# Other estimates and other ranks for the scheduler of a fused transformer kernel

## The chip, the cores and the metric

The kernel runs on one core of a Trainium2 chip. One core has five engines that run their own queues of instructions in order: TensorE (PE, the matrix products), VectorE (DVE), ScalarE (ACT), GpSimd (POOL) and SyncE (SP, which only starts transfers). They meet through semaphores. Sixteen DMA engines move data between the chip's memory and the core. The metric is the device time of one execution in microseconds; of several runs the median is taken.

## The reference

A batch of 16 sequences of 256 tokens of width 128 goes through four layers. Each layer adds a gated cross attention and then a gated feed-forward part to `x`:

```python
x = x + jnp.tanh(g_xattn[0]) * _L0_xattn_ref(_layernorm(x, axis=-1), ctx_1024, ctx_1024, ...)
x = x + jnp.tanh(g_ffn[0]) * _L0_ffn_ref(_layernorm(x, axis=-1), ...)
...
```

- The attentions have 16 heads of width 8 and 64 context tokens. The first takes its softmax over the heads, the others over the context; the second adds a bias for each batch (`fside`) and a mask, the third and the fourth have masks.
- Feed-forward 0 is a mixture of eight experts (128 to 512 to 128, with gelu): each token goes to its two best experts, and a shared expert is added. Feed-forward 1 is a ternary 128x128 matrix. Feed-forward 2 comes down to one expert, the second of its sixteen. Feed-forward 3 is a mixture of eight experts in which each token goes to its best one.

All products are in float32.

## The kernel before

**Halves and stages.** The batch is split in two halves of eight sequences (called half 0 and half 1 here; sequences 0 to 7 and 8 to 15). Each half goes through eight stages: attention 0, mixture 0, attention 1, ternary, attention 2, expert 2, attention 3, mixture 3. The halves share nothing but buffers, so that one half's attention (much DVE work) can run beside the other's mixture (PE and transfers).

**Mixtures.** Tokens are sorted by expert into tiles of 128 rows: 39 tiles for each half in mixture 0 (two experts for a token, and room for a part tile of each expert), 23 in mixture 3. `sorted_pair` (L1901) handles two tiles: fetch the rows (`xg`; in mixture 0 POOL's indirect gather, L1927; in mixture 3 a plain transfer from SP, L1922), transpose them (PE, L1941), copy to `xgT` (DVE, L1945), first product for each tile (PE, L1955), gelu (ACT, L1962), second product (PE, L1976), bias (DVE, L1986), and a store. In mixture 0 the store goes to `ysort` in memory (SP, L2008), from which `collect` (L2036) gathers two rows for each token by POOL (`yg`, L2045) and adds them on DVE (L2053). In mixture 3 an indirect scatter writes the kernel's output (POOL, L2021). `fetch` (L1883) loads each tile's expert, 578 KB, from SP (L1896) into one of six buffers `wb`; a buffer is free when DVE's bias (L1986) of the tile that used it is done.

**Regions.** Mixture 3 scatters the normalised tokens into regions of a table in memory, one for each expert (`last_mixture`, `block`, POOL, L1752), and that table is written with a fill pattern before: `fill_regions` (L1872) issues 27 transfers of 645 KB for each half from SP (L1877). A half's scatters wait for all 27 of its fills. Attention 1 loads its `fside` tile for each sequence in `make_fill1` (L1061, the transfers at L361), also from SP, into one of three buffers. POOL carries small steps of attentions 2 and 3 (`mx`, L1200 to L1203) and of the layer normalisation (`ln`, L738 to L741) as well.

**What sets the order.** No order is written out. Every piece of work is a Python generator that yields requests: `op(engine, length, *needs)`, `dma(queue, size, *needs)` or `get(slots, number, *needs)` for buffers. `Order.run` (L223) takes, again and again, the request that could begin first by its estimates. Begin times are rounded to 0.1 us, and among equal ones the lowest rank wins. The instructions are issued in that order on PE, DVE, ACT, POOL and SP. So the estimates, all in microseconds, decide the order, and nothing of them is executed:

- `REACH` is added where a need comes from another engine; a transfer ends at `max(wire, at + LAND) + size / RATE`, so that all transfers share one wire.
- `RANKS` (L96) has one row for each half and one rank for each of the eight stages; `rank` (L2063) adds a little for each sequence. The shared expert has its mixture's rank plus 0.6, and `collect` its plus 0.1. Constants have rank 50 and the region fills 100.

**Fillers.** Where the scheduler sees PE idle, `keep_busy` (L206) puts in products of the identity whose result nobody reads (`spin`, L471, 128x512 in bfloat16): as many as bring the last 3.4 us of its own timeline to a share of 0.85, each counted as 0.22 us.

```python
                self.wire = max(self.wire, at + LAND) + size / RATE
...
        want = min(room, max(SHARE * min(WINDOW, end) - busy, SHARE * (end - begin - WINDOW)))
        while want > 0 and t < end - SPIN:
            if not self.spin(t):
                return
```

Of the kernel before, what the change touches and what calls it, by code (L numbers as in the profile page):

```python
# [84 lines left out]

PE, DVE, ACT, POOL, SP = "PE", "DVE", "ACT", "POOL", "SP"

REACH, LAND, RATE, SWAP = 0.1, 1.8, 280e3, 1.3
INF = float("inf")


# [1 line left out]

TURNED = (1,)

RANKS = ((4, 10, 2, 10, 1, 7, 1, 16), (15, 10, 3, 16, 5, 13, 12, 16))  # L96


class Event:
# [18 lines left out]
class Order:  # L118
# [33 lines left out]
    def give(self, slot, slots, at):  # L152
        slot.at = at
        slots.free.append(slot)
# [104 lines left out]
def op(engine, length, *needs, table=None):  # L259
    return ("op", engine, length, needs, table)  # L260


def dma(queue, size, *needs):
    return ("dma", queue, size, needs, None)


def get(slots, number, *needs):
    return ("get", slots, number, needs, None)
# [24 lines left out]
def flamingo_kernel(  # L293
# [1028 lines left out]
    def two(slot):  # L1322
        return slot.ap[:, 0:1024].rearrange("p (a b) -> p a b", a=2)
# [82 lines left out]
    def first_mixture(hf, rank, begin, end):  # L1406
# [231 lines left out]
        for q in range((n + 1) // 2):  # L1638
            needs = (indexed, kept)
            order.task(  # L1640
                rank + 0.001 * q,
                sorted_pair(l, hf, q, st, ex, needs, room[q], fetched[q], stored),
            )
# [4 lines left out]
    def last_mixture(hf, rank, begin):  # L1648
# [167 lines left out]
        for q in range((n + 1) // 2):  # L1816
            order.task(
                rank + 0.001 * q,
                sorted_pair(
                    l, hf, q, st, ex, (at, kept), room[q], fetched[q], None, filled, empty  # L1820
                ),
            )
# [78 lines left out]
    def sorted_pair(l, hf, q, st, ex, needs, room, fetched, stored, filled=None, empty=None):  # L1901
# [13 lines left out]
        for i in range(m):  # L1915
            if l == 3:
# [4 lines left out]
                at = yield dma(SP, 132e3)  # L1921
# [3 lines left out]
            at = yield op(POOL, 1.3, *xgs, *needs)  # L1925
# [9 lines left out]
        if l == 0:  # L1935
            at = (at[0] + 3.0, "DMA")
        (xgT,) = yield get(xgT_s, 1)
        (pt,) = yield get(banks, 1)
        pe = at = yield op(PE, 0.11 * m, at, pt)
# [4 lines left out]
        at = yield op(DVE, 0.17 * m, at, xgT)  # L1944
# [4 lines left out]
        hts = []  # L1949
        for i in range(m):  # L1950
            (ph,) = yield get(banks, 1)
            pe = yield op(PE, 0.9, at, ph, fetched)
            for c in range(NF):
                cs = slice(c * P, (c + 1) * P)
                nc.tensor.matmul(  # L1955
                    ph.ap[:, cs], wb[i].ap[:, cs], xgT.ap[:, i * P : (i + 1) * P],
                    start=True, stop=True,
                )
            ht = yield op(ACT, 1.15, pe, hb, table=table)
            for c in range(NF):  # L1960
                cs = slice(c * P, (c + 1) * P)
                nc.scalar.activation(  # L1962
                    two(hb)[:, i, cs], ph.ap[:, cs], func,
                    bias=wb[i].ap[:, PK_B1 + c : PK_B1 + c + 1],
                )
            give(ph, banks, ht)
            hts.append(ht)
# [3 lines left out]
        place = y.ap[:, 2 * D :].bitcast(I32)  # L1971
        (py,) = yield get(banks, 1)
        for i in range(m):
            at = yield op(PE, 0.9, hts[i], py)
            for c in range(NF):
                nc.tensor.matmul(  # L1976
                    py.ap[:, i * D : (i + 1) * D],
                    two(hb)[:, i, c * P : (c + 1) * P],
                    wb[i].ap[:, PK_W2 + c * D : PK_W2 + (c + 1) * D],
                    start=(c == 0),  # L1980
                    stop=(c == NF - 1),
                )
# [23 lines left out]
        if l == 0:  # L2006
            at = yield dma(SP, 65e3 * m, yt)
# [10 lines left out]
        for i in range(m):  # L2018
            at = yield op(POOL, 1.41, yt)
# [10 lines left out]
        at = (at[0] + 3.0, "DMA")  # L2030
# [32 lines left out]
    def rank(stage, hf, i=0):  # L2063
        return RANKS[hf][stage] + 0.01 * i

# [128 lines left out]
```

## Time and profile before

| | |
|---|---|
| median of 14 runs | 1002.89 us (999.21 to 1009.87) |
| the profiled execution | 1006.01 us, of which the span is 1004.3 us |
| PE busy | 916.5 us, 91% of the span |
| DVE, POOL, ACT busy | 666.5, 629.4, 571.4 us |
| mean granted clock of PE | 0.96 |
| transfers | 150.19 MB, 150 GB/s over the span |
| fillers | 175 products |

How to read it: a row of the instruction views gives the start, the duration, the engine, the line in the kernel, what is written and read, the number of merged instructions, and in brackets how long the engine was idle just before and who ended that. Products in the trace are pipelined: the next begins before the one before has ended, so that a duration is longer than the step from one to the next. A row of the stretches gives, for a window of time, the busy time of each engine, the clock granted to PE and what the transfers moved. A float32 product is two entries of the trace.

### The profile page before, as it was taken

What the parts mean: (1) busy time and instruction counts of PE and PEld (TensorE: products, weight loads), DVE (VectorE), ACT (ScalarE), POOL (GpSimd) and SP (SyncE); (2) the same over time, 40 slices, a digit from 0 to 9 for tenths busy, and PEclk for the clock granted to TensorE, in tenths of its full rate; (3) what the DMA queues carried; (4) which work ended last, traced back from release to release, by engine and by line L of the source; (5) the groups of instructions that cost most, each with busy time, mean ns of one, the idle gap of its engine ahead of it and who ended that gap; (6) DMA issues with size and microseconds to landing.
All of it is one profiled execution on the core that took longest, in us unless ns stands there. A gap on an engine that the chain in (4) does not pass through costs nothing.

```text
span 1004.3 us, 28746 instructions
## 1 busy us (share of the span) xinstructions
PE 916.5 (91%) x10775; PEld 719.7 (72%) x10775; DVE 666.5 (66%) x2019; ACT 571.4 (57%) x1359; POOL 629.4 (63%) x1031
## 2 busy tenths in 40 slices
PE   6999968989988999999799989999789999998996
PEld 3777746889876998776567667676566667886875
DVE  5889895574356224578597888789567688765342
ACT  5654324576454446667358558665655776783433
POOL 5798755679762577677458756425286566756443
PEclk9998878999989999999799999999989999999998
DMA  7000004557874689451643940099995014557983
GB/s 212 3 3 24 23 1 143 169 180 232 248 194 164 230 276 351 156 133 46 131 117 83 197 102 2 15 230 219 219 214 136 1 42 162 158 183 266 302 293 124
DMA packets 96428, 150.19 MB, mean 150 GB/s; under 512 B 11298, under 2 KB 75945, under 8 KB 96289
## 3 DMA queue, kind: packets, MB, share of 16 engines
q1 hardware_dynamic: 88304, 131.77, 46.1%
q0 software_dynamic: 7552, 15.65, 6.0%
q8 instruction: 85, 1.39, 0.6%
q10 hardware_dynamic: 432, 0.93, 0.4%
q14 instruction: 55, 0.44, 0.1%
HBM read 99.11 MB, written 50.12 MB: 149 GB/s over the span
## 4 chain that ended last, share of the span: by engine, by line
PE 22%; DVE 7%; SPq 7%; DMA 5%; POOL 4%; issue 3%; ACT 2%; POOLq 0%; DVEq 0%; ACTq 0%
SPq L1877 6%; PE bank L1955 4%; PE bank L1976 3%; DMA xg<-xrow 2%; PE bank L1271 2%; PE bank L1104 2%; DVE mx L1189 2%; DMA yg<-ysort,state 2%; PE bank L1230 2%; PE bank L1293 1%; PE bank L872 1%; DMA xrow<-rows_sb 1%; PE bank L838 1%; PE bank L1238 1%; PE bank L1382 1%
## 5 line engine op out<-in xcount | busy, mean ns | idle before, releaser
L1962 ACT ACTIVATE big<-bank,wb 128x128 f32<-128x128 f32 x496 | 137.4, 384 | 123.1 <-issue 76.0
L1955 PE MATMUL bank<-xgT,wb 128*128 128x128 f32 x992 | 130.9, 281 | 5.7 <-DVE xgT L1945 3.6
L1955 PEld LDWEIGHTS bank<-xgT,wb 128*128 128x128 f32 x992 | 120.7, 195 | 16.8 <-DVE xgT L1945 12.3
L1976 PE MATMUL bank<-wb,big 128*128 128x128 f32 x992 | 125.3, 277 | 0.0
L747 ACT ACTIVATE xn<-x,ln 128x128 f32<-128x128 f32 x224 | 93.7, 492 | 49.9 <-POOL ln L741 49.8
L1976 PEld LDWEIGHTS bank<-wb,big 128*128 128x128 f32 x992 | 119.0, 193 | 1.8 <-issue 0.9
L1927 POOL DMA_INDIRECT xg<-xrow,state x78 | 76.2, 977 | 40.1 <-PE bank L1832 22.6
L1189 DVE TENSOR_REDUCE mx<-bank 128x8 f32<-128x512 f32 x128 | 80.4, 683 | 16.8 <-PE bank L1110 15.9
L1258 ACT ACTIVATE pT<-bank 128x512 f32<-128x512 f32 x128 | 67.2, 606 | 41.1 <-PE bank L1245 38.5
L2045 POOL DMA_INDIRECT yg<-ysort,state x64 | 62.8, 981 | 42.5 <-DVE x L2053 16.9
L990 POOL TENSOR_TENSOR pT<-pT,rc 128x1024 f32<-128x1024 f32 x32 | 75.2, 2373 | 18.8 <-DVE rc L985 14.0
L1986 DVE TENSOR_TENSOR y<-bank,wb 128x128 f32<-128x128 f32 x124 | 32.4, 287 | 80.2 <-PE bank L1976 75.3
L768 POOL TENSOR_TENSOR x<-x,rows_sb 128x256 f32<-128x256 f32 x96 | 71.7, 765 | 14.8 <-ACT xn L747 14.2
L738 POOL TENSOR_SCALAR ln<-ln 128x4 f32<-128x4 f32 x64 | 14.7, 230 | 99.3 <-DVE ln L736 89.4
L2021 POOL DMA_INDIRECT out_dram<-y x46 | 46.8, 1017 | 46.5 <-DVE y L1986 37.2
L735 DVE BATCH_NORM_STATS2 ln<-x 128x6 f32<-128x128 f32 x256 | 68.9, 269 | 5.1 <-DMA x<-in_x_dram 4.8
L1104 PE MATMUL bank<-kexp,qT 32*128 32x256 f32 x768 | 68.4, 415 | 2.2 <-DVE x L1330 2.0
L739 POOL TENSOR_TENSOR ln<-ln,mhalf 128x4 f32<-128x4 f32 x64 | 66.9, 1045 | 5.3
L1945 DVE COPY xgT<-bank 128x256 f32<-128x256 f32 x64 | 25.9, 412 | 58.2 <-PE bank L1941 47.6
L1271 PE MATMUL bank<-pT,vx 128*32 128x256 f32 x768 | 59.0, 395 | 0.2 <-ACT pT L1258 0.2
L736 DVE BATCH_NORM_AGGREGATE ln<-ln 128x2 f32<-128x6 f32 x256 | 46.6, 182 | 9.7
L1142 DVE TENSOR_REDUCE mx<-bank 128x8 f32<-128x512 f32 x64 | 43.5, 682 | 13.6 <-PE bank L1110 13.5
(273 smaller groups left out, 2174.7 us busy)
## 6 DMA issues: line engine op xcount, KB each, us to landing
wb<-in_pk_l_dram SPq DMA_DIRECT2D x124, 578.0 KB
xrow<-rows_sb SPq DMA_DIRECT2D x54, 645.0 KB
xg<-xrow SPq DMA_DIRECT2D x46, 129.0 KB
ysort<-y SPq DMA_DIRECT2D x38, 128.0 KB
fill<-in_fsideT_dram SPq DMA_DIRECT2D x64, 64.0 KB
x<-in_x_dram SPq DMA_DIRECT2D x16, 128.0 KB
xrow<-xn SPq DMA_DIRECT2D x8, 256.0 KB
xg<-xrow,state POOLq DMA_INDIRECT x78
```

The costliest lines, as they stand in the source:

```text
L735: nc.vector.bn_stats(st[:, 2 * i + j, :], xs[b][:, j, :])
L747: nc.scalar.activation(xn[:, k, :], xs[b][:, j, :], AF.Identity, bias=nm[:, k : k + 1], scale=rs[:, k : k + 1],)
L768: nc.gpsimd.tensor_tensor(xs[b], xs[b], row.unsqueeze(1).to_broadcast([P, 2, D]), ALU.add)
L990: nc.gpsimd.tensor_tensor(s3, s3, rc.ap.unsqueeze(1).to_broadcast([P, 8, P]), ALU.mult)
L1104: nc.tensor.matmul(dst(g), qT[strip(g), ts], kexp[strip(g)].rearrange("p h k -> p (h k)"), start=True, stop=False,)
L1189: nc.vector.tensor_reduce(mx[:, :, g, :], sc[g].ap.rearrange("p (t h k) -> p t h k", h=4, k=S2), AX.X, ALU.max,)
L1258: nc.scalar.activation(pTs[g // 2].ap[:, (g % 2) * 512 : (g % 2 + 1) * 512], sc[g].ap, AF.Exp)
L1271: nc.tensor.matmul(po.ap[strip(g), i * S : (i + 1) * S], vx.ap[:, b % 2, c, :], pTs[c // 4].ap[:, (c % 4) * S : (c % 4 + 1) * S], start=Tr ...
L1927: nc.gpsimd.indirect_dma_start(out=xg[i], out_offset=None, in_=xd, in_offset=bass.IndirectOffsetOnAxis(ap=index[:, 2 * q + i : 2 * q + i + ...
L1955: nc.tensor.matmul(ph.ap[:, cs], wb[i].ap[:, cs], xgT.ap[:, i * P : (i + 1) * P], start=True, stop=True,)
L1962: nc.scalar.activation(two(hb)[:, i, cs], ph.ap[:, cs], func, bias=wb[i].ap[:, PK_B1 + c : PK_B1 + c + 1],)
L1976: nc.tensor.matmul(py.ap[:, i * D : (i + 1) * D], two(hb)[:, i, c * P : (c + 1) * P], wb[i].ap[:, PK_W2 + c * D : PK_W2 + (c + 1) * D], st ...
```

## The change

Three things change, all of them numbers that only the scheduler reads. `REACH` goes from 0.1 to 0.3, `LAND` from 1.8 to 2.0 and `RATE` from 280 to 270 KB for each microsecond. The length of a tile's first product in `sorted_pair` goes from 0.9 to 1.0 and of its second from 0.9 to 0.97. Seven of the sixteen ranks change: in half 0 those of attention 0, mixture 0, attention 1 and expert 2, in half 1 those of attention 1, attention 2 and mixture 3. The computation, the buffers, the transfers and their sizes stay as they are; the order of the instructions on each engine and the number and places of the fillers come out otherwise.

```diff
-REACH, LAND, RATE, SWAP = 0.1, 1.8, 280e3, 1.3
+REACH, LAND, RATE, SWAP = 0.3, 2.0, 270e3, 1.3
...
-RANKS = ((4, 10, 2, 10, 1, 7, 1, 16), (15, 10, 3, 16, 5, 13, 12, 16))
+RANKS = ((11, 14, 1, 10, 1, 9, 1, 16), (15, 10, 6, 16, 12, 13, 12, 14))
...
             (ph,) = yield get(banks, 1)
-            pe = yield op(PE, 0.9, at, ph, fetched)
+            pe = yield op(PE, 1.0, at, ph, fetched)
...
         for i in range(m):
-            at = yield op(PE, 0.9, hts[i], py)
+            at = yield op(PE, 0.97, hts[i], py)
```

## The prediction

> **What bounds the kernel now.** First the page, for the engine that is full; then stretches of the span, for where it is not; then the rows around the idle places. The page and the fillers' own line:
>
> ```profile
> PE 916.5 (91%) x10775; PEld 719.7 (72%) x10775; DVE 666.5 (66%) x2019; ACT 571.4 (57%) x1359; POOL 629.4 (63%) x1031
> PEclk9998878999989999999799999999989999999998
> L478 PE MATMUL bank<-ident x175: 376/379/634, 1.4 to 989.5; 128*128 128x512 bf16 x175
> ```
>
> PE is the bound: 87.8 us of the span are not busy, and its clock has a few low slices. What is computed on it does not change, so the change can move three things only: idle PE, stretches at half clock, and fillers. The stretches (columns: busy PE, weight loads, DVE, ACT, POOL with their counts, granted clock, transfer share, GB/s):
>
> ```profile
> 100.00:160.00 60.00, 44.30 (x574) 32.89 (x559) 53.59 (x108) 15.58 (x30) 35.58 (x37) 0.79 0.06 17
> 230.00:300.00 70.00, 62.90 (x664) 57.60 (x663) 28.62 (x99) 38.38 (x112) 54.27 (x65) 0.93 0.73 220
> 300.00:400.00 100.00, 96.22 (x776) 84.66 (x775) 39.42 (x112) 50.24 (x150) 58.78 (x95) 0.98 0.75 253
> 400.00:500.00 100.00, 88.15 (x935) 69.04 (x935) 66.09 (x175) 60.66 (x138) 65.89 (x117) 0.93 0.47 123
> 700.00:760.00 60.00, 51.84 (x713) 36.43 (x712) 38.75 (x126) 35.60 (x79) 33.72 (x68) 0.91 0.94 216
> 890.00:1004.30 114.30, 99.28 (x754) 83.35 (x752) 51.56 (x243) 48.70 (x165) 58.68 (x95) 0.98 0.70 234
> ```
>
> From 100 to 160 DVE is the bound (routing of mixture 0, 53.6 of 60). From 230 to 500 run the experts of mixture 0 and the gathers behind them: 22.7 us of PE idle. At 700 to 760 there is one hole, and after 890 mixture 3 alone, with 15 us idle. The rest is packed. The rows of the two holes, by engine:
>
> ```profile
> 474.98 3.75 SPq L1877 DMA_DIRECT2D xrow<-rows_sb  x4
> 485.03 0.35 DVE L2053 SCALAR_TENSOR_TENSOR x<-yg,state,x 128x128 f32<-128x128 f32 x1 [4.83 <-DMA yg<-ysort,state]
> 486.76 0.95 PE L1168 MATMUL bank<-ident,pT 128*128 128x128 f32 x4 [3.23 <-DVE pT L1150]
> 725.72 1.12 POOL L1752 DMA_INDIRECT xrow<-big,state  x1 [8.82 <-DMA xrow<-rows_sb]
> 730.67 0.40 PE L1212 MATMUL bank<-identb,mx 128*128 128x128 bf16 x2 [6.97 <-POOL mx L1203]
> ```
>
> First hole: four region fills enter the transfer queues at 475, the gathers behind them land late, DVE waits 4.83 us in its order, and PE waits for DVE. Second hole: POOL waits 8.82 us for the regions to be filled, attention 2's small POOL steps stand behind it, PE waits 6.97 us. The rows of the end:
>
> ```profile
> 891.89 0.71 PE L872 MATMUL bank<-wa,oT 128*128 128x128 f32 x4 [0.25 <-ACT oT L1316]
> 918.13 1.00 POOL L1752 DMA_INDIRECT xrow<-big,state  x1 [0.16 <-issue]
> 930.33 1.49 SPq L1922 DMA_DIRECT2D xg<-xrow  x2
> 941.46 2.10 PE L478 MATMUL bank<-ident 128*128 128x512 bf16 x9
> 943.09 1.52 SPq L1896 DMA_DIRECT2D wb<-in_pk_l_dram  x2
> 943.17 0.42 DVE L1945 COPY xgT<-bank 128x256 f32<-128x256 f32 x1
> 943.64 2.05 PE L1955 MATMUL bank<-xgT,wb 128*128 128x128 f32 x16
> 948.06 1.49 SPq L1896 DMA_DIRECT2D wb<-in_pk_l_dram  x2
> 951.67 1.95 PE L1955 MATMUL bank<-xgT,wb 128*128 128x128 f32 x16
> 953.46 2.08 PE L1976 MATMUL bank<-wb,big 128*128 128x128 f32 x16
> 955.74 0.33 PE L1941 MATMUL bank<-ident,xg 128*128 128x128 f32 x1 [0.20 <-DMA xg<-xrow]
> ```
>
> The last attention ends at 892.6, its tokens are scattered by 919.1, and half 1's first rows are fetched at 930.33, since half 0's tiles are still in front in SP's order. A pair of tiles then takes 4.97 us of SP's order (943.09 to 948.06).
>
> **Do the new numbers fit the rows better?** Partly. Two first products begin 1.79 us before the next thing (951.67 to 953.46): 0.895 us for a tile, which is 0.9 and not 1.0. DVE's copy ends at 943.59 and PE begins at 943.64: 0.05 us of way, nearer to 0.1 than to 0.3. Transfers go the other way: the pair whose experts are issued at 948.06 has its rows on PE at 955.74, 7.68 us for 2 x 578 + 2 x 129 KB; the old numbers make 1.8 + 1414/280 = 6.85, the new 2.0 + 1414/270 = 7.24. So three of the numbers move away from the trace and two towards it: this alone decides nothing, and the order must be read.
>
> **The change part by part.** The two sources, built, give the order of every engine (counts, no times). Counts of work are the same on DVE and ACT; POOL issues 4 more separators (L521, 0.21 us each, beside its idle 37%: nothing, or 0.9 us if its queue is full there).
>
> 1. *Fillers before the end of half 1's attention 3*: 83 become 143, and 45 of the 60 stand among mixture 0's experts (32 become 77). In a run a filler steps by (2.10 - 0.38) / 8 = 0.215 us, so 60 cost 12.9 us if PE had no idle there, and nothing if each lies in a wait. The 45 need 9.7 us, and 22.7 us are idle in 230 to 500, but the new ones stand in runs of one to nine at almost every pair, where the old trace shows packed products. I take half: **+6** (0 to 12.9; 15.8 by 46.0 us / 175).
> 2. *Five tiles of half 0's mixture 3 move ahead of the end of attention 3* (first products left behind it: 13 become 8). 5 x 2 x 0.9 = **+9** before that end; from 760 to 890 PE has only 2.1 us idle, so 7 at least.
> 3. *The end after attention 3*: SP's order is 2.5 pairs shorter, 12.4 us, but half 1's rows can't be fetched before their scatters land. They are issued by 919.1, 11.2 us before 930.33, less some 3 us to land: **-8** (0 to -11.2). Fillers there: 92 become 103, 11 x 0.215 = 2.4, in part in waits: **+1**.
> 4. *First hole*: the first fills now stand behind the mask load of the fourth layer's keys (L789, which before waited for ACT until 506) instead of behind half 0's last fside load, and 15 instead of 22 of half 1's gathers are issued after them. The hole costs 3.23 + 2.40 us of waits and 10.2 us at half clock, 10.7 in all. But the next groups of fills are 5 and 9 instead of 3 and 6, 5 x 3.2 us = 16 of transfers before the same loads. I take **-4** (-10.7 to +5).
> 5. *Second hole*: 20 instead of 21 fills stand before half 0's table is full. In the trace they run from 651.58 to 725.72; one less is 3.2 us, so 70.9, and the scatter and the small steps behind it 2 us: 73. PE has 85 steps and 6 fillers between the release of that group and the blocked step, instead of 95 and none: at 75.2/95 = 0.79 us, 68.5, less 3.1 for the loads ahead of the fills, 65.4. The hole is 7.6 us instead of 7.0: **+1** (-7 to +8). What is queued on POOL behind the wait is again an attention's small steps, now of attention 3.
> 6. *Start of mixture 0*: 14 more DVE instructions, 8.6 us by their rows, come before its first bias, in the stretch where DVE is full; PE has 15.7 us idle there and other work: **+2** (0 to 8.6).
>
> Everything else in the order moves work that PE does anyway. Sum: 6 + 9 - 8 + 1 - 4 + 1 + 2 = +7. The profiled execution took 1006.0 us, 3.1 above the median, and so 1013.0 by its own time, **1010 for the median**.
>
> The second hole shows what an idle PE costs beyond itself: from 725.9 to 736.2 the granted clock is 0.5. A rule that speaks against this forecast: the Trainium skill, "TensorE: Matmul & The Clock Gate", section "Why this matters for your kernels", advises against PE gaps of over about 3 us, since an idle window puts the array back to half clock. The trace agrees with it in that row. By the rule the new fillers in mixture 0 would pay: without half clock from 230 to 400, and with their 6 us for nothing, the sum would be about -6.
>
> **The rivals.**
> - *The fillers fall into waits and hold the clock (faster).* Place: mixture 0, 230 to 400. For it: 0.93 and 0.98 granted there, 0.07 x 70 + 0.02 x 100 = 6.9 us lost, and 10.9 us idle. Against it: those low slices come from single waits of up to 3.3 us for gathered rows, not from many short ones. Sum: 7 - 6 - 6.9 = -6, so 997. It decides as soon as fillers cost under 0 net, with term 4 as taken.
> - *The first hole goes (same).* With the gathers clear of the fills all 10.7 us are saved instead of 4: sum 0, 1003.
> - *The larger groups of fills hit attention 1 (much slower).* Nine fills before the fside loads of half 1's last sequences hold them 3 x 3.2 = 9.6 us longer, and a hole of that size costs 5 us of half clock again: 1025. For it: POOL already waits up to 5.5 us for such a load. Against it: those loads wait for buffers (16 us at 554) longer than for the wire.
> - *Nothing changes*: excluded, since the order differs on all engines.
>
> **How the numbers follow.** Forecast 0.45, own range 1006 to 1017; faster rival 0.28; first hole 0.12; larger groups 0.15. Two runs of this kernel can be told apart from about 0.3%, 3 us. Faster 0.28, same 0.12, slower 0.60 (the forecast and the larger groups). The range takes in the faster rival with the first hole half gone as well and the larger groups with term 1 at its bound: 990 to 1030.
>
> **What would show it.** Fillers: busy PE from 230 to 500 up by about the fillers' time, with idle down by less. End: the last L872 near 905 of the span or later, and at most 107 us after it. First hole: no DVE wait of 4 us for `yg` beside a group of L1877, and clock 1.0 from 487 to 497. Second hole: one POOL wait for `xrow` of 8 to 10 us and one PE wait of 7 to 8. The forecast is wrong if idle PE outside the end falls by more than the 13 us of new fillers, or if a new hole of over 5 us stands in attention 1.

## The result and the profile after

The changed kernel takes 1039.37 us (median of 13 runs, 1035.87 to 1043.53), the kernel before 1005.09 us (median of 62 runs); the ratio is 1.0346, with an interval of 1.0325 to 1.0367. The forecast was 1010 with a range of 990 to 1030: the sign is right, and the loss of about 34 us is five times the 7 us of the sum. The profiled execution of the changed kernel spans 1036.1 us, 31.7 more than before.

The page after, in its rows of busy time and granted clock and in the fillers' own row:

```profile
PE 942.6 (91%) x10846; PEld 739.0 (71%) x10846; DVE 674.9 (65%) x2019; ACT 570.0 (55%) x1359; POOL 627.1 (61%) x1035
PEclk9999779998999999999889989999999999999998
L478 PE MATMUL bank<-ident 128*128 128x512 bf16 x246 | 67.4, 396 | 1.6 <-POOL hmask L403 1.4 <-DVE pT L1150 0.2
```

PE's share is 91% as before, and its busy time has grown by 26.1 us, of which 21.4 carry the name of the fillers. A first reading is that the fillers ate the time. The experiments below refute it: when the fillers are taken out, the time stays.

The same six stretches as in the prediction (busy PE, weight loads, DVE, ACT, POOL with counts, granted clock, transfer share, GB/s); the last runs to the new end:

```profile
100.00:160.00 60.00, 45.42 (x595) 32.48 (x595) 55.15 (x112) 21.09 (x37) 35.00 (x37) 0.80 0.13 39
230.00:300.00 70.00, 64.39 (x582) 56.01 (x583) 32.15 (x92) 34.14 (x100) 53.90 (x64) 0.93 0.74 228
300.00:400.00 100.00, 92.88 (x726) 81.39 (x724) 34.38 (x103) 46.61 (x145) 49.23 (x82) 1.00 0.68 224
400.00:500.00 100.00, 89.54 (x891) 72.79 (x895) 64.19 (x170) 59.91 (x139) 71.39 (x118) 0.94 0.57 152
700.00:760.00 60.00, 56.80 (x696) 40.44 (x689) 48.06 (x148) 37.70 (x82) 21.27 (x44) 1.00 1.11 222
890.00:1036.05 146.05, 130.59 (x1146) 110.64 (x1144) 71.63 (x315) 75.30 (x220) 77.94 (x129) 0.97 0.67 215
```

Clock times shift, so stretches between equal clock times compare different work. A better comparison counts the pieces of work that the scheduler gives to PE, in order (992 in each kernel, fillers left out; the first product of a tile is one piece, for example), and takes the start of the piece with the same number in both traces. The orders differ, so the work behind a number isn't always the same, and pieces differ in length: a few us of the lead can be other work. The lead of the kernel before, in us:

| piece | 160 | 240 | 400 | 440 | 680 | 720 | 880 | last product of attention 3 | end of span |
|---|---|---|---|---|---|---|---|---|---|
| after less before | -4 | +4 | +12 | +12 | +32 | +23 | +31 | +40 | +32 |

The last tile of mixture 0 is piece 401 before and 388 after; from 440 to 680 stand the attentions of both halves, with the last gathers of half 1. There the loss is largest. From piece 400 to piece 600 both kernels do nearly the same work on PE (2039 entries of the trace before, 2026 after, and 7 and 21 fillers). The two stretches, before and then after, columns as above:

```profile
458.60:635.40 176.80, 164.05 (x2046) 116.18 (x2044) 141.32 (x420) 113.52 (x245) 113.67 (x219) 0.97 0.43 95
```

```profile
470.90:665.00 194.10, 173.97 (x2047) 124.40 (x2047) 140.25 (x398) 109.00 (x233) 114.94 (x218) 0.94 0.39 85
```

The 17.3 us more are, by estimate, 7.4 of idle PE (176.80 - 164.05 = 12.75 becomes 194.10 - 173.97 = 20.13) and some 6 of lower clock (0.03 x 176.8 = 5.3 becomes 0.06 x 194.1 = 11.6); 14 more fillers make another 3. What PE waits for is seen in the rows of SP, DVE and PE, in order of time:

```profile
480.98 0.35 SPq L789 DMA_DIRECT2D xf<-in_mask_dram  x1
481.38 4.02 SPq L1877 DMA_DIRECT2D xrow<-rows_sb  x4
522.21 5.00 SPq L1877 DMA_DIRECT2D xrow<-rows_sb  x5
584.79 17.36 SPq L1877 DMA_DIRECT2D xrow<-rows_sb  x9
```

```profile
492.30 0.35 DVE L2053 SCALAR_TENSOR_TENSOR x<-yg,state,x 128x128 f32<-128x128 f32 x1 [4.93 <-DMA yg<-ysort,state]
534.96 0.35 DVE L2053 SCALAR_TENSOR_TENSOR x<-yg,state,x 128x128 f32<-128x128 f32 x1 [3.75 <-DMA yg<-ysort,state]
602.02 0.35 DVE L2053 SCALAR_TENSOR_TENSOR x<-yg,state,x 128x128 f32<-128x128 f32 x1 [5.18 <-DMA yg<-ysort,state]
```

```profile
494.45 1.09 PE L1293 MATMUL bank<-ident,ov 128*128 128x128 f32 x4 [4.61 <-DVE pT L1150]
536.03 1.12 PE L1042 MATMUL bank<-wa,ctx_sb 128*64 128x128 f32 x8 [3.12 <-DVE x L1330]
604.48 0.69 PE L1313 MATMUL bank<-ident,o 128*128 128x128 f32 x2 [4.96 <-DVE o L1302]
```

Three groups of region fills, and behind each a gather of half 1 that lands late, DVE standing in its order, and PE standing for DVE. In the kernel before only one wait of PE behind such a gather is over 3 us. The chain of waits of the changed kernel (start, length) names the same three gathers, right behind the groups:

```profile
487.11 10.44 DMA yg<-ysort,state
524.61 10.33 DMA yg<-ysort,state
591.62 10.38 DMA yg<-ysort,state
```

The second hole of the kernel before is gone. POOL's first scatter into the regions, the row below, now waits 3.73 us instead of 8.82, no wait of PE from 721 to 764 is over 0.5 us, and the stretch from 700 to 760 above has clock 1.00:

```profile
761.07 1.13 POOL L1752 DMA_INDIRECT xrow<-big,state  x1 [3.73 <-DMA xrow<-rows_sb]
```

The end: the last product of attention 3 begins here, and the span ends 103.7 us after its end (before: 111.7).

```profile
931.72 0.61 PE L872 MATMUL bank<-wa,oT 128*128 128x128 f32 x4
```

### The profile page after: what moved, and what is told of

It reads as the page before. It is cut to its first block, busy times and chain, and to the rows that moved or that the text cites. A ratio compares the mean times of both kernels' runs of the same rounds, so it can differ in the third digit from the quotient of the medians.

```text
span 1036.1 us, 28865 instructions
## 1 busy us (share of the span) xinstructions
PE 942.6 (91%) x10846; PEld 739.0 (71%) x10846; DVE 674.9 (65%) x2019; ACT 570.0 (55%) x1359; POOL 627.1 (61%) x1035
## 4 chain that ended last, share of the span: by engine, by line
PE 44%; DVE 16%; DMA 14%; POOL 10%; SPq 6%; issue 6%; ACT 4%; POOLq 0%; DVEq 0%; ACTq 0%
PE bank L1955 7%; PE bank L1976 6%; DMA xg<-xrow,state 5%; SPq L1877 5%; DMA yg<-ysort,state 3%; PE bank L1104 3%; PE bank L1271 3%; PE bank L1846 3%; PE bank L1230 2%; PE bank L1832 2%; POOL pT L990 2%; POOL xg L1927 2%; DVE mx L1189 2%; DMA xg<-xrow 2%; PE bank L478 2%
## 5 line engine op out<-in xcount | busy, mean ns | idle before, releaser
L1976 PEld LDWEIGHTS bank<-wb,big 128*128 128x128 f32 x992 | 121.3, 194 | 6.9 <-issue 2.4
L1189 DVE TENSOR_REDUCE mx<-bank 128x8 f32<-128x512 f32 x128 | 80.8, 682 | 15.9 <-PE bank L1110 14.6
L1104 PE MATMUL bank<-kexp,qT 32*128 32x256 f32 x768 | 76.0, 435 | 1.7 <-DVE mx L1189 1.0
L768 POOL TENSOR_TENSOR x<-x,rows_sb 128x256 f32<-128x256 f32 x96 | 68.6, 732 | 8.5 <-ACT xn L747 7.8
L478 PE MATMUL bank<-ident 128*128 128x512 bf16 x246 | 67.4, 396 | 1.6 <-POOL hmask L403 1.4
L1271 PE MATMUL bank<-pT,vx 128*32 128x256 f32 x768 | 56.9, 387 | 0.0
L1230 PE MATMUL bank<-qT,kexp 32*128 32x256 f32 x512 | 56.1, 406 | 0.6 <-DVE mx L1189 0.6
```

Of the source, the lines that this page charges most:

```text
L478: nc.tensor.matmul(bank.ap.rearrange("p (a b) -> p a b", a=2), data[:, 0:P], data.unsqueeze(1).to_broadcast([P, 2, 2 * P]), start=True, st ...
L1104: nc.tensor.matmul(dst(g), qT[strip(g), ts], kexp[strip(g)].rearrange("p h k -> p (h k)"), start=True, stop=False,)
L1189: nc.vector.tensor_reduce(mx[:, :, g, :], sc[g].ap.rearrange("p (t h k) -> p t h k", h=4, k=S2), AX.X, ALU.max,)
L1230: nc.tensor.matmul(dst(g), kexp[strip(g), 2 * i : 2 * i + 2, :].rearrange("p h k -> p (h k)"), qT[strip(g)], start=True, stop=False,)
L1271: nc.tensor.matmul(po.ap[strip(g), i * S : (i + 1) * S], vx.ap[:, b % 2, c, :], pTs[c // 4].ap[:, (c % 4) * S : (c % 4 + 1) * S], start=Tr ...
L1976: nc.tensor.matmul(py.ap[:, i * D : (i + 1) * D], two(hb)[:, i, c * P : (c + 1) * P], wb[i].ap[:, PK_W2 + c * D : PK_W2 + (c + 1) * D], st ...
```

## The experiments

Each ratio is to the kernel before on the same chip. The chips differ, so the time of the kernel before on that chip stands with each group. Theory A says that the fillers cost their time on PE's path; the rival (theories B and S in the expectations), that the waits of the order cost it. The kernels without fillers leave out only products that nobody reads.

### Do the fillers cost the time?

The fillers' products are left out of both kernels; the scheduler still counts them, so that the order stays.

```diff
-        data = ident.bitcast(BF16)
-        nc.tensor.matmul(
-            bank.ap.rearrange("p (a b) -> p a b", a=2), data[:, 0:P],
-            data.unsqueeze(1).to_broadcast([P, 2, 2 * P]), start=True, stop=True,
-        )
         return True
```

The changed kernel without them:

> The changed kernel with its order kept and all 246 fillers left out (what they compute is never read). Theory A, the added fillers lie on the path: the changed kernel loses 246 x 0.215 = 53 us of filler time less what they cover and less the clock they hold; against the same edit on the kernel before (e2) the distance shrinks from 34 to about 34 - 15 = 19 us. Theory B, the fillers stand in waits that are there anyway and the order alone costs the 34 us: the distance between e1 and e2 stays at 34 us.

The kernel before without them:

> The kernel before with its order kept and its 175 fillers left out (nothing that is computed reads them). If its fillers stand in waits: no gain, and some us lost to stretches at half clock, 1005 to 1020. If they lie on the path: up to 175 x 0.215 = 38 us faster, 967 to 1000.

Measured (before: 1054.6): 1.0214 [1.0148, 1.0279] and 1.0029 [0.9992, 1.0067]. Without one filler in either, the two orders are 1079.4 - 1055.8 = 23.6 us apart. That lies between the 19 us of theory A and the 34 of theory B and decides nothing by itself, as the changed kernel with its fillers was not run on this chip; on the next one its distance is 28.7 us.

The changed kernel itself, and the same without the 77 fillers among mixture 0's experts, which term 1 of the prediction charged most:

```diff
+        order.fillers = getattr(order, "fillers", 0) + 1
+        if 34 < order.fillers <= 111:
+            return True
```

> The changed kernel itself, beside the runs below on one chip: 1.03 to 1.04 times the kernel before. All theories expect that; it is the measure for the next three.

> The changed kernel, its order kept, without the 77 fillers that stand among mixture 0's experts (nothing reads what they compute). Theory A (fillers on the path): 77 x 0.215 = 16.6 us faster than the changed kernel, 0.98 to 0.99 of it. Theory B (they lie in waits): the same time within 3 us, or slower by the half clock that returns.

Measured (before: 1053.8): 1.0256 [1.0185, 1.0327] and 1.0280 [1.0209, 1.0351]: no gain, where theory A had 16.6 us. From piece 160 to 400 the trace takes 268.9 us with these fillers and 265.8 without, of which PE is idle for 30.0 and for 37.7.

### The ranks or the numbers?

The new ranks with the old numbers, and the new numbers with the old ranks:

```diff
-RANKS = ((4, 10, 2, 10, 1, 7, 1, 16), (15, 10, 3, 16, 5, 13, 12, 16))
+RANKS = ((11, 14, 1, 10, 1, 9, 1, 16), (15, 10, 6, 16, 12, 13, 12, 14))
```

> The kernel before with the new ranks and the old lengths. Its order has 395 fillers, 316 of them before the end of half 1's attention 3 (83 in the kernel before). Theory A: 233 x 0.215 = 50 us more at most, 1030 to 1060. Theory B: what the ranks make of the order alone counts; the same ranks are in the changed kernel, so near its 1039, 1025 to 1045.

> The changed kernel with the old ranks: new REACH, LAND, RATE and tile lengths alone. 308 fillers, 146 of them before the end of half 1's attention 3, 162 after it; no tile of half 0's mixture 3 is left for the time in which half 1's last tokens are sorted. Theory A: 63 x 0.215 = 14 us before that end, and a longer end, 5 tiles x 2 us less to fill it with: 1015 to 1040. Theory B with the ranks as the cause: near 1005. If the old ranks fit only the old numbers: over 1030.

Measured (before: 1054.6): 1.0794 [1.0713, 1.0875] and 1.0238 [1.0173, 1.0304]. The ranks alone are worst, and beyond what either theory gave them (at most 1060 where the kernel before takes 1005, a ratio of 1.055); the numbers alone lie inside the range of theory A. On top of the new numbers the ranks cost next to nothing (1.0238 against 1.0256 for both, on another chip). The parts don't add up.

### The collision of fills and gathers

Half 0's 27 fills are issued during attention 0, where the transfers have little to do, and the first seven of half 1 with its eighth. The order on the other engines stays.

```diff
         at = yield from project(0, b, oT, biased[0, b], at)
         order.set(X[1][b], at)
+        if b < 7:
+            fill_early(b)
...
             at = yield dma(SP, 4.0 * P * m * ROW3, whens[i * m * len(whens) // n])
-            nc.sync.dma_start(
+            if hf == 1 and i >= 7:
+                for k in range(0 if i == 7 else i, i + 1):
+                    fill_one(xd, k)
```

> The changed kernel with the same order on PE, DVE, ACT and POOL; only SP issues half 0's 27 region fills early, while attention 0 runs and the transfers idle, and the first seven of half 1's with the eighth. Theory C: the groups of fills at 481, 522 and 585 us of the changed kernel's trace hold the gathers of mixture 0's results (10 us each in the chain of waits) and that is the part of the loss that fillers do not explain. Then the changed kernel gains 15 to 30 us, and the same move gains less in the kernel before (e8), so that their distance shrinks from 34 to under 20. If the loss comes from the order on the engines: equal gains in both, and the distance stays.

> The kernel before with the same move of the fills. Both of its holes hang on the fills (the DVE wait for the gathers at 485, POOL's wait for full regions at 717), each with some 5 us of half clock behind it: 10 to 25 us faster, 0.975 to 0.99. If the transfers are hidden anyway or the early fills hold up the first loads: 0.995 or more.

Measured (before: 1053.8): the changed kernel 1.0228 [1.0154, 1.0301], the kernel before 1.0007 [0.9970, 1.0043]. In the trace the changed kernel wins 11.4 us from piece 440 to piece 560 (117.7 becomes 106.3) and loses 7 before piece 160. So the collision is real, and 11 us large on this chip. The kernel before comes out even. The distance between the two orders falls from 28.7 to 24.4 us, where theory C had it under 20: with the collision gone they are still 2.2% apart. The collision is a part of the loss and not all that separates the kernels.

### What do the numbers say, and does it matter?

Four kernels with the old ranks, each with one edit of the numbers. The first changes one length by 0.4%, and can hardly be called a better or worse estimate:

```diff
-REACH, LAND, RATE, SWAP = 0.1, 1.8, 280e3, 1.3
+REACH, LAND, RATE, SWAP = 0.1, 1.8, 279e3, 1.3
```

> The kernel before with one number moved by 0.4%: a transfer's rate of 279 instead of 280 KB for each microsecond. 168 fillers instead of 175, and another order of the instructions on every engine from the experts of mixture 0 on. Theory N (the new numbers are worse lengths, and the loss grows with how far they stand from the trace): a ratio of 1.000, at most 1.003. Theory O (the time follows from the accidents of the order, and most orders near the old one are worse, whatever is written in the numbers): 1.010 to 1.030. Theory A (fillers on the path): 7 fillers fewer, no loss, 0.999.

The second, the third and the fourth do one part of the change each: `REACH` 0.3; the tile's two lengths; `LAND` 2.0 and `RATE` 270.

> The kernel before with REACH 0.3 alone. 323 fillers (90 among the experts of mixture 0, 177 after attention 3), no tile of half 0's mixture 3 left behind the last attention. Theory N: REACH moves away from the row (0.05 us measured) and brings most of the loss of all numbers together: 1.015 to 1.025. Theory O: 1.010 to 1.030 without an order among the three single edits. Theory A: 148 more fillers at 0.215 us are 32 us, 1.030.

> The kernel before with the tile's products at 1.0 and 0.97 alone. 165 fillers. Theory N: a length 0.1 above the row, less weight than REACH: 1.003 to 1.010. Theory O: 1.010 to 1.030 again. Theory A: 10 fillers fewer, 0.998.

> The kernel before with LAND 2.0 and RATE 270 alone. 217 fillers. Theory N: these two move towards the row (7.68 us for a pair's transfers; 6.85 by the old numbers, 7.24 by the new): 0.990 to 1.000. Theory O: 1.010 to 1.030 again. Theory A: 42 more fillers, 9 us, 1.009.

Measured (before: 995.5):

| edit | fillers | time, us | ratio |
|---|---|---|---|
| `RATE` 279 | 168 | 1025.05 | 1.0305 [1.0255, 1.0355] |
| `REACH` 0.3 | 323 | 1059.39 | 1.0647 [1.0601, 1.0693] |
| lengths 1.0 and 0.97 | 165 | 1029.21 | 1.0362 [1.0312, 1.0413] |
| `LAND` 2.0, `RATE` 270 | 217 | 1025.26 | 1.0299 [1.0252, 1.0346] |

Moving one number by 0.4% costs as much as moving two of them towards the trace, and about as much as the whole change. Theory N, by which a worse length gives a worse order, falls with the first row and the last. Theory O comes nearest, though `REACH` and the lengths go beyond its 1.010 to 1.030: what the edit does is to shuffle the order, and all seven shuffled orders that were run (these four, the ranks alone, the numbers alone, the whole change) are 2.4 to 7.9% slower than the old one. With `RATE` 279 a part of the loss stands where the changed kernel has none. No trace of the kernel before is kept from this chip; beside the first one, only 18.2 of the 29.5 us that are lost on the chip show, and the places hold for that part alone. Up to piece 640, counted every 40 pieces, its trace is never more than 2.5 us behind the one of before. From piece 680 to 720 it takes 51.0 instead of 44.4 us, around the second hole, which this order keeps: a group of 35 fills, a scatter of POOL that waits for them, and behind it this time not the small steps of attention 2 but the mask tile of attention 3 (`fillb`, made on POOL at L1080). Another 7 us are added from piece 720 to 880. Its rows of SP, POOL and PE around the second hole:

```profile
673.03 97.84 SPq L1877 DMA_DIRECT2D xrow<-rows_sb  x35
```

```profile
732.05 1.12 POOL L1752 DMA_INDIRECT xrow<-big,state  x1 [9.88 <-DMA xrow<-rows_sb]
```

```profile
737.03 0.29 PE L1110 MATMUL bank<-id32b,fillb 32*128 32x128 bf16 x4 [6.41 <-POOL fillb L1080]
```

### Both kernels on one chip, and the fillers once more

In the table the time grows with the fillers, by (1059.4 - 1029.2) / (323 - 165) = 0.19 us for each, close to a filler's step of 0.215 us. That is what theory A would predict on these quicker chips, so it was tried again, with the orders that have most of them.

> The kernel before itself, for a profile on the chip of its neighbours in this group: a ratio of 1.000, within 0.3%. It is what the next three are compared with, stretch by stretch.

> The changed kernel once more, on another chip: every theory 1.025 to 1.037.

> The changed kernel without its 246 fillers (they compute nothing that is read), on a chip where the kernel before may be near 1000 us again; it was 1.0214 where that took 1055. Theory A (a filler costs its step of 0.215 us on the path): 53 us less than the changed kernel, 0.98. Theory S (a filler stands where the scheduler counts PE idle, and PE is idle there in a run too; fillers are a sign of an order with waits, not their cause): within 0.5% of the changed kernel, 1.025 to 1.035.

> The kernel with REACH 0.3 alone, which had 323 fillers and 1.065, without those fillers. Theory A: 323 x 0.215 = 69 us less, 0.995. Theory S: 1.055 to 1.068. Between them each filler's cost on the path is (1.065 - ratio) x 1000 / 323 us.

Measured (before: 1062.4): 1.0004 [0.9972, 1.0036]; 1.0242 [1.0152, 1.0333]; without its fillers 1.0259 [1.0203, 1.0316]; `REACH` alone without fillers 1.0369 [1.0319, 1.0419], under the 1.055 to 1.068 of theory S and far from the 0.995 of theory A; it has no partner with fillers on that chip. With both kernels on one chip, the leads can be set beside those of the two first traces, for which the record names no chip (us gained or, with a plus, lost by the changed kernel in each stretch of pieces):

| pieces | 0 to 160 | 160 to 400 | 400 to 440 | 440 to 680 | 680 to 720 | 720 to 880 |
|---|---|---|---|---|---|---|
| the two first traces | -4 | +16 | 0 | +19 | -9 | +8 |
| on this one chip | -10 | +10 | +4 | +16 | +2 | +15 |

The losses among mixture 0's experts (160 to 400), from 440 to 680 and from 720 to 880 are there on both; the size of the second hole isn't steady.

The pair that settles the fillers, on a chip where the kernel before takes 1004.1 us:

> REACH 0.3 alone with its 323 fillers, beside the next on one chip. 1.0647 where the kernel before took 996 us; where that takes 1055 or more, the changed kernel's loss was 0.7 of what it was, so 1.045.

> The same without the 323 fillers (they compute nothing that is read). Theory A (each costs 0.215 us): 69 us less than the one beside it. Theory S (they stand in waits that stay): within 10 us of it. A part between the two gives the price of a filler on the path, the difference by 323; 1.0369 on a chip where the kernel before took 1062 us would be 8 us less than 1.045, 0.03 us for each.

Measured: 1.0654 [1.0626, 1.0682] with the 323 fillers, 1.0687 [1.0659, 1.0716] without. The pages, with and then without:

```profile
PE 960.1 (90%) x10923; PEld 742.3 (70%) x10923; DVE 672.6 (63%) x2019; ACT 599.7 (56%) x1381; POOL 626.8 (59%) x1022
PEclk9998789999999999999968989998999999999899
```

```profile
PE 912.2 (85%) x10600; PEld 724.3 (68%) x10600; DVE 673.4 (63%) x2019; ACT 599.9 (56%) x1381; POOL 627.2 (59%) x1022
PEclk9999779999889999998968989998999999986798
```

PE's busy time falls by 47.9 us and the span grows by 4.8 (1066.7 to 1071.5). At one place it can be seen what happens: where the one trace has a run of 71 fillers, the other has a hole of about the same length, until the same rows land (rows of PE, with and then without; without, the line numbers are five lower, L1936 for L1941).

```profile
978.65 15.49 PE L478 MATMUL bank<-ident 128*128 128x512 bf16 x71
997.05 1.53 PE L1941 MATMUL bank<-ident,xg 128*128 128x128 f32 x4 [2.90 <-DMA xg<-xrow]
```

```profile
1001.89 1.19 PE L1936 MATMUL bank<-ident,xg 128*128 128x128 f32 x3 [17.28 <-DMA xg<-xrow]
```

Theory A falls here too. The scheduler puts a filler where its timeline has PE idle, and PE is idle there on the chip as well: many fillers are the sign of an order with many waits. In this pair they even pay a little, 3.3 us; the mean granted clock is 0.951 with them and 0.923 without.

## Why the prediction was wrong, step by step

The step that failed is the sentence under the sum, "Everything else in the order moves work that PE does anyway", which priced the whole reordering at nothing. The last product of attention 3 ends 39.7 us later, where the terms ahead of it (6 + 9 - 4 + 1 + 2) made 14. PE up to the end of that product, all of its rows and then the fillers alone (busy PE, the other engines where the row has them, clock, transfer share, GB/s), before and after:

```profile
0.00:892.60 892.60, 819.49 (x10037) 637.82 (x10037) 617.24 (x1787) 524.08 (x1197) 570.72 (x936) 0.96 0.51 139
0.00:892.60 892.60, 23.85 (x83) 8.44 (x83) 0.96 0.51 139
```

```profile
0.00:932.33 932.33, 853.55 (x10186) 663.72 (x10186) 629.62 (x1809) 529.39 (x1223) 573.77 (x949) 0.96 0.51 136
0.00:932.33 932.33, 41.28 (x143) 14.80 (x143) 0.96 0.51 136
```

Idle PE grows by 5.7 us (73.1 becomes 78.8), and the rows of the fillers, which stand in waits by the runs without them, by 17.4, in part beside other products. So up to 23 of the 39.7 us are waits, where the sum had 5 (6 - 4 + 1 + 2); about 9 are the five tiles, and what is left are the same products taking longer, at the same mean clock of 0.96. Of the waits only those behind the three gathers are traced to their cause; the rest stays open.

1. *Fillers, +6.* Wrong. No comparison with and without them shows a cost beyond its interval: 1.0256 and 1.0280 (77 of them), 1.0242 and 1.0259 (246), 1.0654 and 1.0687 (323). The lower end given, nothing, was the value.
2. *Five tiles ahead, +9.* About right. The end of attention 3 is piece 908 instead of 895, and from piece 880 to it the lead grows by 39.7 - 30.7 = 9.0, on the one chip by 13.4.
3. *The end, -8 and +1.* Right: 103.7 us instead of 111.7, so -8.0 with the fillers there; on the one chip 106.9 instead of 121.4.
4. *First hole, -4.* Wrong in mechanism. The mask load, said to hold the fills until about 506, went at 480.98, and the fills at 481.38. In the trace of before it waited for ACT until 506, and that time was taken over into the new order as if it were fixed. The hole stays at its place (from piece 400 to 440 the lead stays at +12), and the next groups, of 5 and 9, make two more like it. Of the rivals, the one with the larger groups came nearest, and its price (9.6 us and 5 of half clock) was of the size that the early fills gave back (11.4); but it had the victims wrong. They are not the loads of `fside` but half 1's gathers, which in the new order come later and so meet those groups.
5. *Second hole, +1.* Wrong: it is gone, -8.6 from piece 680 to 720. POOL's wait is 3.7 us. The fills end later than before, but POOL reaches the scatter only at 757.3, where it had stood there from 716.9.
6. *Start of mixture 0, +2.* Wrong in sign, small: from piece 40 to 120, which holds that stretch, the changed kernel gains 1.9 us in the first pair of traces (123.9 becomes 122.0) and 3.2 on one chip (128.5 becomes 125.3).

The loss among mixture 0's experts (+16 and +10) was in the sum only as fillers. They lie in it, but the time stays without them (1.0256 with, 1.0280 without). It and the loss from 720 to 880 (+8 and +15) were not traced to single waits; from 720 to 880, 25 instead of 16 of the 160 pieces are of mixture 3's tiles, so that a part of it can be their work. Nor is it known why the old order is better than each of its neighbours, or whether its ranks and numbers were chosen for each other; shown is only that it is, for the seven tried.

On the clock the prediction set a rule of the Trainium skill, "TensorE: Matmul & The Clock Gate", section "Why this matters for your kernels", against its own term: no idle gaps of PE over about 3 us, or the clock falls to half. The runs agree in sign and not in size. The clock does fall without the 323 fillers, from 0.951 to 0.923, but the time grows by 0.3% only. That PE has nothing urgent to do in those stretches would explain it and was not tried by itself. Nor did the new fillers hold the clock where the rival expected it: from piece 160 to 400 both first traces are at half clock for 17.1 us.

## What to carry to other kernels

Where a scheduler's estimates decide an order, price the order and not the estimates: here a change of 0.4% in one number cost 3%, so each new order has to be read for waits, and the forecast of an unread one needs a range of several per cent upwards. Fillers are a gauge of the idle time that a planner expects: before they are charged as work, ask what PE would do at that moment without them. When a transfer or a load is argued to be held by something, follow that something into the new order too.

## What the runs showed of the hardware

A gather took four times as long beside bulk stores, though the two are in different queues. In the changed kernel's trace, transfers issued from 440 to 470 us, with no fills, and then from 480 to 500, beside four fills (queue that issues, number, us to landing, which the trace has for one gather of each window; the three of the chain above waited 10.3 to 10.4):

```profile
yg<-ysort,state POOLq DMA_INDIRECT x11, 2.6
```

```profile
yg<-ysort,state POOLq DMA_INDIRECT x7, 11.1
```

The Trainium skill, "DMA: Bandwidth & Descriptors", section "Queues, rings and completion order", says that a transfer engine goes round its queues after each packet. By that rule a gather waits for a packet of the fills at each turn. In the trace's packet records the 16 packets of 4 KB of the gather issued at 482.34 us start between 486.61 and 490.01 and take 0.2 to 0.4 us each: the time is lost ahead of its packets. Whether such turns make it up, no run here shows.

With the fills early, PE also stood still for no reason that the profile names while the transfers were full: from 20 to 100 us it has 5.0 and 2.7 us of waits put down to "issue", and the stretch from 48 to 93 has a transfer share of 0.98. With the fills at their usual place no such wait is among the longest there; that run (e5) has some elsewhere, five of 0.3 to 0.9 us between 433 and 440 us, at a transfer share of 0.77. The cause was not tried.

The chips differed by up to 6.7%. The kernel before took 995.5 and 1004.1 us on two chips of the experiments and 1053.8 to 1062.4 on three. The difference is mostly in mixture 0's experts; the same pieces of PE's work, with the same transfers, on the chip of the profile before and on one of the slower ones:

```profile
312.70:458.60 145.90, 137.50 (x1221) 119.58 (x1220) 66.43 (x187) 83.03 (x226) 99.24 (x162) 0.98 0.67 217
```

```profile
326.10:503.50 177.40, 147.04 (x1221) 126.65 (x1220) 66.24 (x194) 84.82 (x231) 99.90 (x163) 0.93 0.56 179
```

31.5 of the 53 us between the two traces lie here, at 179 instead of 217 GB/s. The change costs 3.5% where the kernel before takes 1005 us and 2.4 to 2.6% where it takes 1054 or 1062; whether the slower transfers hide a part of it was not tried by itself.
